# Four graph layers in one launch: where layer 1 builds the row sums for layer 2

## The chip, the cores and the metric

The kernel runs on one core of one Trainium2 chip. The metric is the device time of one launch in microseconds (us), of the slowest core, which here is the only one. Three runs of the kernel before the change took 2272.49 to 2273.15 us, with a median of 2272.7 us.

## What is computed

The input is a matrix `x` of 3327 rows of 256 numbers and an integer matrix `adj` of 3327 x 3327, of which only "greater than zero" matters. Four layers follow each other, each with a residual and a layer norm. The masked softmax over the rows of `adj` is in each of them.

```python
def _L1_gnn_ref(x, adj, W, a):
    h = x @ W
    e = (h @ a[:D, 0])[:, None] + (h @ a[D:, 0])[None, :]
    e = jnp.where(e > 0, e, 0.01 * e)
    attention = jax.nn.softmax(jnp.where(adj > 0, e, -1e12), axis=1)
    return jax.nn.elu(attention @ h)

def _L2_gnn_ref(x, adj, Wq, bq, Wk, bk, Wv, bv):
    q, k, v = x @ Wq.T + bq, x @ Wk.T + bk, x @ Wv.T + bv
    scores = q @ k.T / jnp.sqrt(d)
    attention = jax.nn.softmax(jnp.where(adj > 0, scores, -9e15), axis=-1)
    return jax.nn.elu(attention @ v)

x = _layernorm(x + _L0_gnn_ref(x, adj, Wq, Wk))       # cosine attention
x = _layernorm(x + _L1_gnn_ref(x, adj, W, a))
x = _layernorm(x + _L2_gnn_ref(x, adj, Wq, bq, Wk, bk, Wv, bv))
x = _layernorm(x + _L3_gnn_ref(x, adj, W0, W1, a1, W2, a2, W3, a3))
```

(The function bodies are shortened. Layer 0 normalizes queries and keys instead of scaling the scores. Layer 3 multiplies by `W0` and then runs three layers like layer 1, with `W1, a1` to `W3, a3`.) The change touches layer 1, the start of layer 2, and one place in layer 0.

## The kernel before

**Tiles and passes.** The rows of `x` are cut into 26 tiles of 128 rows, taken as 13 pairs. Six passes run: layers 0, 1 and 2, and the three parts 3a, 3b, 3c of layer 3. Each pass goes through seven column blocks `b`, six of four output tiles (512 columns) and a last one of two, and in each block through all 26 tiles `j`. So a step of the main loop is (layer, block, tile). In a step, ScalarE (ACT) and VectorE (DVE) make the attention weights of one tile against the block's 512 columns; TensorE (PE) multiplies them with the rows of that tile and adds the product up in five PSUM banks called `po`. In layer 1 and in 3a to 3c the weights are `re` (ACT, L786) and then `ft` or `e` (DVE, L799).

**Seven products in place of eight.** In the blocks that `strassen(L, b)` names, two tiles (a pair `p`) are multiplied by seven products of half size in place of eight (`products`, matmul at L942). Each needs four sums of the weights (`ssum`, `qsum`) and four sums of the pair's rows. The latter are the row sums of this text. `combine(key, p, v)` makes the four sums `t1` to `t4` of pair `p` for layer `key` with four VectorE operations, beside a column of ones that adds up the softmax denominator, and a DMA on SyncE's queue (SP) writes them to DRAM, `t_d[key][p]`. `fetch_tsum` (L860) loads them again for every block that uses them, into one of three buffers called `tsum`. The rows of layer 2 are the output of layer 1, so `combine("2", p)` runs inside layer 1, block by block.

**The end of a block.** When the last tile of a block has been added up, the banks are emptied: `joined` copies one of the products on ACT (`p<-po`, L968) and adds the others on DVE (`zs` L974 to L977, `p` L980 to L986). Then `finish` divides, turns the result (`planes<-p`, L1001, two copies on ACT that split the 32 bits into two planes of 16; a DMA transpose, L1004, on SP; copies of the turned planes, L1015), projects it (L1207), applies the elu (L1219), adds the residual (`y`, L1225 and L1234), and takes the layer norm. In layer 1 the normed rows come out in `o4` (L1270, on ACT) and go back into the tiles `v` of the next layer over DMAs.

**What follows it in layer 1.** In the other passes what follows is part of the block's own chain; in layer 1 it is put into a queue called `tail`, from which the main loop takes one step after each tile: `combined()`, which calls `combine("2", p)` for the two pairs of the block with a step after each and one empty step at its end; then `turn(o4, ...)`, which makes `planes<-o` on ACT (L1001), a DMA transpose on SP and, for the first four blocks, writes the turned rows to DRAM (`tr_d`, L1011), from where `turned_again` fetches them (L1029) late in layer 1 as the keys `FT` of layer 2; then `followed()`.

**Buffers.** Buffers are taken by tag, and a new user of a tag waits until an earlier one is free. Tag `x4k` has two buffers, which the `tsum` of `combine("2")` shares with the `planes` and a few others. Tag `stage` has four, `po` five banks. Tags `w_l0_wqk` and `row_1` hold the query and key weights of layer 0 and a vector of layer 1; in layer 2 two of the `ksum` tiles (pairs 1 and 2) lie there, and later weights of 3b.

**The start of layer 2.** `sum_keys(p)` (L627 to L630) makes four sums of a pair's keys, `ksum`, on DVE: some of them ahead of need, at the steps listed in `KSTEPS`, the others two steps before the pair's weights (`make`). `pair_weights` (L647 to L674) multiplies them with the sums of the queries. `masked` (L494) is the DVE operation that multiplies the finished weights of layer 2 by the mask. `weights2` (L684, L692) makes the weights of layer 2's tiles that aren't taken by pairs.

**Who sets the order.** A scheduler puts the instructions of every engine in one order, by what each depends on and by the priorities of the program; each engine then works through its own in that order and waits where an operand is missing. `tc.issue_after(i)` places what is issued in it behind instruction `i`.

## Time and profile before

The profiled execution is not one of the three runs. Its numbers beside theirs, and the stretches of the three layers concerned:

| what | value |
|---|---|
| median of three runs | 2272.7 us |
| the profiled execution | 2275.28 us |
| its span, first to last instruction | 2273.5 us |
| its mean granted TensorE clock | 0.994 |
| layer 0, 0 to 513 us: PE busy | 510.19 us |
| layer 1, 513 to 801 us: PE busy | 268.07 of 288 us |
| first 287 us of layer 2: PE busy | 285.73 us |
| `re<-u,nrh,th`, L786, ACT, all | 728 x 776 ns = 531.4 us with its smaller shapes |
| `planes<-o`, L1001, ACT | 14 x 981 ns, 19.0 us idle before them |
| `p<-po`, L968, ACT | 30 x 358 ns, 9.3 us idle before them |
| `ksum<-ft`, L627, DVE | 37 x 282 ns, 3.6 us idle before them |

How to read the views: The page gives for every engine the time in which it was busy; PEld is TensorE's loading of weights, which overlaps its matmuls. A table of stretches gives, for each stretch of time, its length and every engine's busy time with the number of instructions, then PEclk, the TensorE clock that was granted (1.00 is full speed), the busy share of the DMA engines and their rate. A line of the timeline gives start, duration, engine, source line, operation, output <- inputs, shape and number, and in brackets how long the engine stood idle before it and what ended that idle time. A line of waits gives who waited for whom, the sum, how often, and the longest. `v`, `ft`, `tsums`, `po` and so on are the program's names for tiles.

### The profile page before, as it was taken

How to read it: one execution, taken by the hardware profiler on the slowest of the kernel's cores; microseconds unless marked ns; L12 is line 12 of the kernel's file. 1: busy time of each engine (PE TensorE's matmuls, PEld its weight loads, DVE VectorE, ACT ScalarE, POOL GpSimd, SP SyncE). 2: the span in 40 equal slices, each digit the busy share in tenths (PEclk: the TensorE clock that was granted, in tenths of full speed). 3: DMA queues.
4: the chain of work that ended last, by engine and by line, in shares of the span. 5: the costliest groups of instructions: out<-in, count | busy, mean ns of one | idle time of the engine just before them, and what ended most of it. 6: DMA issues, size and time to landing. Idle time of an engine off the chain costs nothing. (4 is left out here: it accounts for less than half of the span.)

```text
span 2273.5 us, 43942 instructions
## 1 busy us (share of the span) xinstructions
PE 2225.7 (98%) x16053; PEld 2040.7 (90%) x16053; DVE 2023.7 (89%) x5495; ACT 1368.9 (60%) x2317; POOL 88.7 (4%) x256
## 2 busy tenths in 40 slices
PE   9999999999999899999999999999999999999997
PEld 7788888889999789999999999999999999899997
DVE  6789999988888778988988989999898999899997
ACT  4677777775666645445444445766565765665663
POOL 0000001000000000000000000000000000000000
PEclk9999999999999999999999999999999999999999
DMA  8655665646665622133132244656545556455542
GB/s 276 197 178 168 196 192 190 187 135 154 176 175 139 167 80 82 47 96 91 48 94 81 64 143 153 156 145 169 139 112 161 152 141 161 109 164 164 152 121 56
DMA packets 217037, 318.84 MB, mean 140 GB/s; under 512 B 95870, under 2 KB 125301, under 8 KB 212213
## 3 DMA queue, kind: packets, MB, share of 16 engines
q1 hardware_dynamic: 207908, 307.90, 46.8%
q0 software_dynamic: 8640, 7.87, 2.4%
q8 instruction: 127, 2.08, 0.4%
q14 instruction: 90, 0.73, 0.1%
q10 hardware_dynamic: 272, 0.26, 0.0%
HBM read 243.97 MB, written 40.54 MB: 125 GB/s over the span
## 5 line engine op out<-in xcount | busy, mean ns | idle before, releaser
L786 ACT ACTIVATE re<-u,nrh,th 128x512 f32<-128x512 f32 (+1 forms) x728 | 531.4, 776 | 194.5 <-DVE ft L799 160.7
L942 PE MATMUL po<-tsums,qsum 128*128 128x128 f32 (+1 forms) x3240 | 457.0, 277 | 13.3 <-ACT p L968 4.4
L799 DVE SCALAR_TENSOR_TENSOR ft<-re,rh,mask 128x512 f32<-128x512 f32 x598 | 433.5, 742 | 9.4 <-ACT re L786 7.5
L942 PEld LDWEIGHTS po<-tsums,qsum 128*128 128x128 f32 x3240 | 410.0, 194 | 15.3 <-ACT p L968 11.3
L942 PE MATMUL po<-v,ft 128*128 128x129 f32 x2392 | 365.2, 276 | 0.6 <-DVE ft L799 0.6
L942 PE MATMUL po<-tsums,ssum 128*128 128x128 f32 (+1 forms) x2142 | 326.7, 275 | 5.7 <-DMA tsums<-t_d 1.8
L942 PEld LDWEIGHTS po<-v,ft 128*128 128x128 f32 x2392 | 321.6, 192 | 5.5 <-DVE ft L799 1.0
L942 PEld LDWEIGHTS po<-tsums,ssum 128*128 128x128 f32 x2142 | 295.1, 192 | 21.5 <-issue 5.0
L942 PEld LDWEIGHTS po<-v,e 128*128 128x128 f32 x1196 | 169.3, 191 | 35.6 <-issue 23.9
L1695 PE MATMUL po<-v,e 128*128 128x257 f32 x832 | 194.2, 384 | 5.1 <-DVE zs L977 3.9
L1695 PEld LDWEIGHTS po<-v,e 128*128 128x128 f32 x832 | 157.5, 191 | 37.6 <-issue 8.9
L522 ACT ACTIVATE ex<-ps,rq 128x512 f32<-128x512 f32 (+1 forms) x183 | 118.8, 651 | 114.0 <-PE ps L509 110.9
L942 PE MATMUL po<-tsums,ft 128*128 128x128 f32 x1196 | 184.4, 276 | 0.0
L942 PE MATMUL po<-v,e 128*128 128x129 f32 x1196 | 182.3, 275 | 0.0
L509 PE MATMUL ps<-ft 128*128 128x512 f32 (+1 forms) x364 | 167.1, 564 | 0.1
L942 PE MATMUL po<-v,qsum 128*128 128x128 f32 x1080 | 165.3, 276 | 0.0
L942 PEld LDWEIGHTS po<-tsums,ft 128*128 128x128 f32 x1196 | 159.3, 193 | 0.1
L494 DVE SCALAR_TENSOR_TENSOR e<-ex,mask 128x512 f32<-128x512 f32 (+1 forms) x182 | 118.2, 650 | 41.5 <-ACT ex L674 16.5
L942 PEld LDWEIGHTS po<-v,qsum 128*128 128x128 f32 x1080 | 143.0, 193 | 0.0
L523 DVE SCALAR_TENSOR_TENSOR e<-ex,mask 128x512 f32<-128x512 f32 (+1 forms) x183 | 116.1, 642 | 27.8 <-ACT ex L522 27.4
L465 DVE CUSTOM_DVE_ANT_0 acc<-acc,stage 128x1024 uint16<-128x1024 uint16 (+1 forms) x168 | 108.4, 645 | 10.9 <-DMA stage<-in_adj_a 9.0
L647 PE MATMUL ps<-gsums,ksum 128*128 128x256 f32 x408 | 112.4, 382 | 1.0 <-ACT ex L658 0.7
(332 smaller groups left out, 3752.7 us busy)
## 6 DMA issues: line engine op xcount, KB each, us to landing
tsums<-t_d SPq DMA_DIRECT2D x217, 256.5 KB
mask<-mask_d SPq DMA_DIRECT2D x30, 1664.0 KB
stage<-in_adj_a SPq DMA_DIRECT2D x78, 512.0 KB
tsums<-t3a_d SPq DMA_DIRECT2D x77, 256.5 KB
tsums<-t3b_d SPq DMA_DIRECT2D x77, 256.5 KB
tsums<-t3c_d SPq DMA_DIRECT2D x77, 256.5 KB
mask_d<-mask SPq DMA_DIRECT2D x6, 1664.0 KB
xsum<-v POOLq DMA_DIRECT2D x60, 128.0 KB, 4.3
```

The costliest lines, as they stand in the source:

```text
L465: nc.vector.tensor_tensor(acc, acc, st[:, h * wd : (h + 1) * wd], ALU.add)
L494: nc.vector.scalar_tensor_tensor(e[:, :wd], t_[:, :wd], 0.0, mask(b, j), ALU.add, ALU.mult)
L509: nc.tensor.matmul(ps[:, :wd], FT[j // 4][:, 0, (j % 4) * P : (j % 4 + 1) * P], FT[b][:, 1, :wd], start=True, stop=True,)
L522: nc.scalar.activation(t_[:, c], ps[:, c], AF.Exp, scale=rq[:, j : j + 1])
L523: nc.vector.scalar_tensor_tensor(e[:, c], t_[:, c], 0.0, mask(b, j)[:, c], ALU.add, ALU.mult)
L647: nc.tensor.matmul(out, l, r, start=first, stop=True, skip_group_check=True)
L786: a_ = nc.scalar.activation(t_[:, :wd], self.u[b][:, :wd], AF.Relu, bias=self.nrh[:, j : j + 1], scale=self.th[:, j : j + 1],)
L799: v_ = nc.vector.scalar_tensor_tensor(e[:, :wd], t_[:, :wd], self.rh[:, j : j + 1], mask(b, j), ALU.add, ALU.mult,)
L942: nc.tensor.matmul(o, x, y, start=(p == 0 and g not in banks[:i]), stop=(p == NT // 2 - 1 and g not in banks[i + 1 :]),)
L1695: nc.tensor.matmul(pos[k], e[:, k * P : (k + 1) * P], V[L.i % 2][i], start=(i == 0), stop=(i == NT - 1),)
```

## The change

It has three parts.

1. The row sums of layer 2, except those of the last pair (which stay on chip), take their buffers from the tags `w_l0_wqk` and `row_1` in turn, and not from `x4k`. The order inside is now `t2, t3, t4, t1`, ones, so that the column of ones comes last, for all layers. The buffer holds only the four sums, and the DMA writes only these; the ones of the twelve pairs are written into `t_d["2"]` once, by twelve DMAs of 128 x 1 numbers that are issued in block 3 of layer 0. The memset of the ones on DVE is left out; the last pair's goes to GpSimd (POOL).
2. The empty step at the end of `combined()` is left out, so that `turn(o4)` begins a step sooner.
3. The key sums of layer 2's block 0, both those of `KSTEPS` and those made two steps ahead, are placed behind the last mask multiplication (`masked`) that was issued before them.

```diff
@@ -488,10 +488,12 @@
         nc.vector.tensor_scalar(am[:, :n], am[:, :n], 0.0, 0.5, ALU.is_gt, ALU.mult)
         anyadj[b] = am
 
+    last_masked = [None]
+
     def masked(b, j, t_):
         wd = bw(b)
         e = work.tile([P, CH], F32, tag="e", name="e", bufs=9)
-        nc.vector.scalar_tensor_tensor(
+        last_masked[0] = nc.vector.scalar_tensor_tensor(
             e[:, :wd], t_[:, :wd], 0.0, mask(b, j), ALU.add, ALU.mult
         )
         return e
@@ -833,25 +835,28 @@
 
         b1, b2 = v[2 * p], v[2 * p + 1]
         b11, b12, b21, b22 = b1[:, H:D], b1[:, :H], b2[:, H:D], b2[:, :H]
-        if (key, p) in kept or key in ("0", "1"):
+        if key == "2" and (key, p) not in kept:
+            t = wts.tile([P, 4 * H], F32, tag=("w_l0_wqk", "row_1")[p % 2], name="tsum")
+        elif (key, p) in kept or key in ("0", "1"):
             t = work.tile([P, 4 * H + 1], F32, tag="tsum", name="tsums", bufs=3)
         else:
             t = work.tile([P, 4 * H + 1], F32, tag="x4k", name="tsum", bufs=2)
         if (key, p) in kept:
             tsums[kept[key, p], p] = t
-        t1, t2, t3, t4 = (t[:, c : c + H] for c in (0, H + 1, 2 * H + 1, 3 * H + 1))
+        t2, t3, t4, t1 = (t[:, c : c + H] for c in range(0, 4 * H, H))
         if e is None:
-            (nc.vector if key == "2" else nc.gpsimd).memset(t[:, H : H + 1], 1.0)
+            if key != "2" or (key, p) in kept:
+                nc.gpsimd.memset(t[:, 4 * H :], 1.0)
             nc.vector.tensor_tensor(t1, b12, b11, ALU.subtract)
             nc.vector.tensor_tensor(t3, b22, b12, ALU.subtract)
         else:
-            one = t[:, H : H + 1]
+            one = t[:, 4 * H :]
             nc.vector.tensor_scalar(one, e[:, :1], 0.0, None, ALU.is_ge)
             nc.vector.scalar_tensor_tensor(t1, b12, one, b11, ALU.mult, ALU.subtract)
             nc.vector.scalar_tensor_tensor(t3, b22, one, b12, ALU.mult, ALU.subtract)
         nc.vector.tensor_tensor(t2, b22, t1, ALU.subtract)
         nc.vector.tensor_tensor(t4, t2, b21, ALU.subtract)
-        nc.sync.dma_start(t_d[key][p], t)
+        nc.sync.dma_start(t_d[key][p][:, : t.shape[1]], t)
 
     fetched = [None]
 
@@ -920,10 +925,10 @@
             1: b1[:, H:],
             2: b2[:, H:],
             3: b2[:, :H],
-            4: t[:, 3 * H + 1 :],
-            5: t[:, : H + 1],
-            6: t[:, H + 1 : 2 * H + 1],
-            7: t[:, 2 * H + 1 : 3 * H + 1],
+            4: t[:, 2 * H : 3 * H],
+            5: t[:, 3 * H :],
+            6: t[:, :H],
+            7: t[:, H : 2 * H],
         }
 
         for k, i in (
@@ -1309,7 +1314,6 @@
                 for k in range(0, n, 2):
                     combine("2", (ts_[0] + k) // 2, {t: o4[:, i, :] for i, t in enumerate(ts_)})
                     yield
-                yield
 
             if L.key == "1":
                 if b < NB - 1:
@@ -1502,7 +1506,8 @@
         if j % 2 == 0 and s + 2 < len(steps):
             ln, bn, jn = steps[s + 2]
             if by_pairs(ln, bn, jn // 2) and jn // 2 not in ksum:
-                now[bn, jn // 2] = sum_keys(jn // 2)
+                with tc.issue_after(last_masked[0].ins) if bn == 0 else ExitStack():
+                    now[bn, jn // 2] = sum_keys(jn // 2)
         done = inner.popleft() if j % 2 and inner else None
         if done:
             next(done)
@@ -1736,6 +1741,8 @@
         begin = 14
         if L.is_gat and b < NB - 1:
             begin = 2 if last and b == NB - 2 else 10
+        if L.key == "0" and b == 3 and j < NT // 2 - 1:
+            nc.sync.dma_start(t_d["2"][j][:, 4 * H :], ones[:, :1])
         if L.key == "0" and b == NB - 1 and j % 6 == 0 and 0 < j < 24:
             combine("1", j // 6 - 1, V[1])
         if L.key == "1" and j % 4 == 1 and j < (24, 12, 0, 0, 0, 0, 0)[b]:
@@ -1749,7 +1756,8 @@
                         again.remove(g)
         if L.key == "2" and b * NT + j in KSTEPS:
             p = KSTEPS[b * NT + j]
-            ksum[p] = sum_keys(p)
+            with tc.issue_after(last_masked[0].ins):
+                ksum[p] = sum_keys(p)
         if L.key == "2" and (b, j) == (0, 3):
             sum_queries(0)
         if j == (25 if L.key == "1" else 22) and not end:
```

## The prediction, made before the changed kernel was run

> **What bounds the kernel now.** I read the page first, then the table of stretches, then TensorE's waits, then the timeline around the longest of them, and last the groups by line.

> ```profile
> PE 2225.7 (98%) x16053; PEld 2040.7 (90%) x16053; DVE 2023.7 (89%) x5495; ACT 1368.9 (60%) x2317; POOL 88.7 (4%) x256
> ```

> TensorE (PE) is busy for 98% of the span, so only work taken from it, a gap in it, or a slow clock can change the time. No matmul is added or removed. The gaps are 47.8 us in all, so I looked for those the change can touch: layer 1, from about 513 to 790 us.

> ```profile
> core 0: us, PE busy (x) PEld busy (x) DVE busy (x) ACT busy (x) POOL busy (x), PEclk, DMA share, GB/s
> 563.34:613.78 50.44, 47.10 (x388) 46.36 (x389) 43.21 (x107) 31.40 (x46) 3.13 (x4) 0.97 0.65 175
> 613.78:663.34 49.56, 46.68 (x384) 45.92 (x385) 43.40 (x106) 31.79 (x46) 2.57 (x3) 0.97 0.66 170
> 663.34:710.51 47.17, 44.34 (x380) 43.76 (x381) 43.17 (x106) 31.49 (x46) 4.29 (x5) 1.00 0.65 164
> 710.51:760.90 50.39, 46.51 (x375) 45.46 (x375) 39.65 (x102) 28.92 (x45) 2.58 (x3) 0.97 0.67 169
> 760.90:801.18 40.28, 36.71 (x134) 26.21 (x135) 31.20 (x119) 28.23 (x45) 2.58 (x3) 0.96 0.53 144
> ...
> 1501.15:1545.36 44.21, 44.21 (x384) 43.77 (x383) 42.18 (x97) 29.22 (x46) 3.64 (x6) 1.00 0.61 164
> ...
> 1797.09:1842.70 45.61, 45.60 (x393) 44.98 (x393) 43.02 (x99) 29.77 (x47) 3.63 (x6) 1.00 0.63 153
> ```

> The first four rows are full column blocks of layer 1, cut where TensorE restarts after a block change. The last two are blocks of layers 3a and 3b with the same products. Layer 3a needs 44.21 us; layer 1 needs 47 to 50.

> ```profile
> PE po L942 <- ACT p L968: 4.4, 2, 2.8
> PE po L1695 <- DVE zs L977: 3.9, 1, 3.9
> PE po L942 <- DVE p L980: 3.4, 1, 3.4
> PE po L942 <- DVE zs L977: 2.8, 1, 2.8
> PE po L942 <- DMA tsums<-t_d: 1.8, 2, 1.3
> ```

> These are TensorE's waits from 540 to 765 us. Four rows, 14.5 us, wait for the same thing: a bank of the finished block (`po`) that ScalarE (ACT) must copy (L968) and VectorE (DVE) must add to before the next block may write it. The timeline shows why that copy is late:

> ```profile
> 559.07 0.83 PE L942 MATMUL po<-v,ft 128*128 128x129 f32 x6
> ...
> 560.40 1.99 ACT L1001 COPY planes<-o 128x1024 uint16<-128x1024 uint16 x2 [4.20 <-DMA t_d<-tsum]
> ...
> 562.29 0.36 ACT L968 COPY p<-po 128x256 f32<-128x256 f32 x1
> ...
> 563.34 1.76 PE L942 MATMUL po<-tsums,qsum 128*128 128x128 f32 x8 [3.43 <-DVE p L980]
> ```

> The next fence is the same place of a block change in layer 3a, and the one after it a stretch of one microsecond after the change near 611 us, with the columns of the table above.

> ```profile
> 1504.99 0.37 ACT L968 COPY p<-po 128x256 f32<-128x256 f32 x1 [0.59 <-PE po L942]
> ...
> 1507.24 0.83 PE L942 MATMUL po<-v,ft 128*128 128x129 f32 x6
> ```

> ```profile
> 616.00:617.00 1.00, 1.00 (x6) 1.00 (x6) 1.00 (x3) 0.80 (x2) 0.00 (x0) 0.50 1.07 186
> ```

> ACT stands in order. `planes<-o` waits 4.20 us because its slot (tag `x4k`, two buffers) is still being read by the DMA that writes `tsum` to DRAM. The L968 copy stands behind it. In layer 3a no such copy is in front: L968 runs 2.25 us before the next block's first matmul, and TensorE has no gap. The same picture repeats near 610, 661, 708 and 757 us, with TensorE gaps of 2.83, 1.56, 2.83 and 3.88 us. The row at 616 shows a second cost: after the gaps at 560, 610, 708 and 757 the granted clock is 0.50 for 3 to 4 us, some 1.5 to 1.9 us lost each; after the 1.56 us gap it stays 1.00.

> **The change, part by part.**

> *Places of their own for layer 2's row sums.* `planes<-o` loses its DMA wait (19.0 us of ACT idle time in the group's row, six times). In the built order it also stands two to five `re` activations earlier, ahead of L968. ACT has room: before 560 us it sat idle for 2.18 us ahead of the last two `re`. So L968 should start when its bank is complete, as in layer 3a. First block change: minus 3.43. The four periods sum to 197.56 us. What an unblocked one takes is bounded by 44.21 (3a) and 45.61 (3b, which holds a transfer wait). Layer 1 has its own measure: the third row started without a slow clock, and 47.17 less its final gap of 2.83 is 44.34. The first two rows, less gap, tsums wait (0.51, 1.31) and 1.75 of clock, give 45.35 and 44.94. I take 44.9: 197.56 - 179.6 = 18.0 us gained, bounds 15.1 (all at 45.61) and 20.7 (all at 44.21). VectorE fits: 43.4 us of work per block, as in layer 3a, so it nearly becomes the bound.

> *The last block of layer 1* (760.90 to 801.18). It is only two tiles wide, so TensorE has little to do while the finished block runs L968, `planes<-p`, transpose, `pT`, projection: L968 at 759.81 to the first projection at 774.35 is 14.5 us, and VectorE and ACT pace it. L968 cannot start before five more `re` of 0.6 us, about 2 us after the last full block's end (754.4) instead of 5.4, so up to 2.7 us of the 3.88 gap may stay. But one `elu_e` now stands one 1.3 us copy earlier on ACT, and VectorE no longer holds key sums in this stretch (one stood 2.88 us waiting for a copy of `ft`, with the others about 5 us of work). The gain is between 0 and 6.5 us (TensorE's own work here is 33.8 us); I take 3.0, nearer the lower end because the chain, not TensorE, paces it.

> A gap left at that change has a price in clock: the 2.83 us gaps were each followed by 3 us at 0.50, so I count 1.6 us for a gap of 2.7, inside the 3.0. [...]

> *Planes a step sooner.* One empty step is gone per block. It issues two ACT copies (0.99 us each) and one DMA transpose on SP sooner; that transpose now stands before the next fetches of `tsums`, one or two places earlier in SP's order. SP's transposes take 1.24, 2.08 and 5.27 us (least, median, most). The fetch behind it went out at 556.89 for a pair needed 3.1 us after the block change, 563.0: a lead of 6.1 us against a landing of about 2.7 (fetch at 604.0, TensorE released at 606.7). At 2.08 us it is hidden, at 5.27 it costs 2 us. I take 0; the 44.9 leaves 0.5 for it.

> *Key sums behind the weights.* About 32 VectorE additions (0.28 us, 0.2 apart) move from 770-794 into layer 2's first block. From 800 to 840 VectorE was busy 30.5 of 40 us, partly idle because ACT waited on planes (3.45 and 1.94 us idle). It stays under 40, so 0, bounds -1 to +2. TensorE's wait of 0.78 us for L692 at 814 us, also behind planes, should go: 0.3 net.

> *Memsets.* Twelve of 0.06 us leave VectorE and one moves to POOL (0.1 us, 4% busy): 0.

> *Ones in DRAM.* Twelve DMAs of 128 x 4 bytes on SP. The built order puts them among layer 0's adjacency loads near 60 to 75 us, and one load falls behind two stores of row sums, about 4 us. TensorE shows 60.00 of 60 us busy there although VectorE waited 3.6 us for such loads: covered. I take 0; the bounds are 0 and 12 x 4.3 us (the `xsum` DMA's landing time, the only one shown) = 51.6, if they ran one by one and nothing covered them.
> [...]

> Sum: 3.4 + 18.0 + 3.0 + 0.3 = 24.7 us. The profiled execution took 2275.3 us (span 2273.5), 2.6 above the median of 2272.7; taken from the median: **2248 us**.

> **Rivals.**

> *Fetches late behind the moved transposes.* For: SP is in order, and at the first and fourth block change three fetches stand behind the transpose. Against: median 2.08 us. At 2 us on each of five changes the gain is 14.7: 2258.

> *The last block gives time back.* For: its chain is longer than TensorE's work. If the 3.0 is nothing and 2.7 us of gap with 1.6 of clock come on top of today's waits, the gain is 17.4: 2255.

> *Slower: the twelve DMAs starve layer 0.* At the full 51.6 us, less some 19 us that the four buffers of loads cover (a load each 4.7 us), 32.6 reach TensorE: 2272.7 - 24.7 + 32.6 = 2281. It decides only from 24.7 us past the cover. Against: nothing suggests that these run one by one; the loads on the same queue overlap.

> *It doesn't do what it says:* `planes` waits for another user of its slot, and L968 stays late: 2272. Against: the slot's earlier users finish 10 us or more before.

> **How the numbers follow.** Forecast 0.66, late fetches 0.14, last block 0.12, slower 0.04, no effect 0.04. The forecast's own range: gains of 18 (15.1 + 3.4, nothing else) to 30 (20.7 + 3.4 + 6.5, less 1), 2242 to 2255. Reaching to the first rival and some of it beyond: 2242 to 2261. About 0.2% (4.5 us) is what a measurement can tell from no change; the cases give 0.92 faster, 0.04 same, 0.04 slower.

> **What would show it.** Right: `planes<-o` with no wait for `t_d<-tsum`; L968 before the block's last matmul; layer 1 periods of 44 to 46 us; granted clock 1.00 through them; first layer 2 products about 24 us earlier. Wrong: TensorE waiting on `tsums<-t_d` for over 1.5 us at the changes, a gap over 2 us before the projection in the last block, or gaps before 120 us.

## The result, and the profile after

| | before | after |
|---|---|---|
| median | 2270.5 us (12 runs, 2266.5 to 2275.9) | 2264.6 us (12 runs, 2260.3 to 2269.6) |
| profiled execution | 2275.3 us | 2264.4 us |
| ratio after / before | | 0.9973, 95% interval 0.9961 to 0.9984 |

The change makes the kernel 3.6 to 8.9 us faster. The forecast was 24.7 us, a time of 2248.0 us in a range of 2242 to 2261.

What the change was to remove is gone. The row of the planes' group, all layers, before (L1001) and after (L1006), gives busy time, mean ns of one, and the idle time before them:

```profile
L1001 ACT COPY planes<-o 128x1024 uint16<-128x1024 uint16 (+1 forms) x14 | 13.2, 981 | 19.0 <-DMA t_d<-tsum 19.0
```

```profile
L1006 ACT COPY planes<-o 128x1024 uint16<-128x1024 uint16 (+1 forms) x14 | 13.1, 976 | 0.0
```

TensorE's waits from 540 to 765 us in the profile after (who waited for whom, us in total, times, longest):

```profile
PE po L947 <- DMA tsums<-t_d: 10.5, 8, 2.3
PE pproj L1212 <- DVE pT L1020: 2.0, 1, 2.0
```

`planes<-o` waits for nothing (19.0 us before), and no wait for a bank of the finished block is left (14.5 us before). In their place TensorE waits eight times, 10.5 us, for row sums fetched from DRAM, for which it waited 1.8 us before. The new kernel's lines are five further down after the changed functions: L942 is L947, L968 is L973, L1015 is L1020, L1288 is L1293. Blocks are counted from 0, as in the program, and a place is written block.pair. Block 0 of layer 1 isn't taken by pairs and runs before the 513 us from which the tables count layer 1; blocks 1 to 5 are taken by pairs, and block 6 is the narrow last one. The "first block change" is the one from block 1 to block 2.

Both programs issue the same 16053 matmul records, in nearly the same order, so the same record can be compared in both. The table of stretches below is cut at such records: the first two rows are before, from TensorE's start in block 2 to a matmul early in layer 1's last block (the one that waited 3.88 us before the change, so that this gap lies in the first row), and from there well into layer 2 (pair weights running); the other two are the same work after.

```profile
563.34:760.90 197.56, 184.63 (x1527) 181.50 (x1527) 169.44 (x418) 123.59 (x183) 12.58 (x15) 0.97 0.66 170
760.90:838.15 77.25, 72.90 (x358) 56.78 (x359) 59.20 (x205) 45.39 (x79) 2.58 (x3) 0.98 0.41 110
```

```profile
560.42:752.81 192.39, 181.85 (x1528) 178.50 (x1527) 170.52 (x414) 122.31 (x185) 13.75 (x16) 0.99 0.69 177
752.81:827.86 75.05, 72.21 (x359) 56.89 (x358) 53.38 (x173) 44.69 (x78) 1.72 (x2) 0.98 0.40 110
```

| step of the sum | forecast | measured in the two profiles |
|---|---|---|
| up to layer 1 (twelve DMAs of ones) | 0 | -0.7 |
| first block change | 3.4 | 3.6 |
| four block periods | 18.0 | 197.56 - 192.39 = 5.2 |
| last block, and L692 in layer 2 | 3.3 | 77.25 - 75.05 = 2.2 |
| the rest of the kernel | 0 | 0.3 |
| sum | 24.7 | 10.6 |

The step that failed is the periods. Why a fetch is late shows in the timeline of SP and ACT after, near 650 us, with TensorE's wait behind it:

```profile
646.20 2.06 ACT L1275 ACTIVATE o<-y,nm,rstd 128x256 f32<-128x256 f32 x4
646.81 2.03 SPq L1293 DMA_DIRECT2D v<-o  x2
...
648.95 0.53 SPq L865 DMA_DIRECT2D tsums<-t_d  x1
...
652.27 0.98 PE L947 MATMUL po<-tsums,ssum 128*128 128x128 f32 x3 [2.28 <-DMA tsums<-t_d]
```

The fetch of pair 3.12 needs a buffer, which TensorE freed at 642.6 us (the last matmul of pair 3.9 on `tsums`). It goes out at 649.5. Between the two, SP stands at the stores of the normed rows `v<-o`, which wait for ACT's `o` (L1275). TensorE uses a pair up in 3.1 us, and with three buffers a fetch that leaves at once is out 6.9 us before TensorE wants it (pairs 3.10 and 3.11). This one was out 0.5 us before TensorE wanted it (649.99), and TensorE started 2.8 us after the issue. In the profile before, the stores stand at the same place in SP's order. After the change TensorE wants pair 3.12 6.6 us sooner (656.63 before), but ACT begins `o` only 4.8 us sooner (650.98), and the fetch is out only 3.9 us sooner.

A second kind of lateness, near the first block change, first before and then after:

```profile
556.89 0.43 SPq L860 DMA_DIRECT2D tsums<-t_d  x1
562.41 2.01 SPq L1004 DMA_TRANSPOSE turned<-planes  x1
```

```profile
554.07 1.04 ACT L1006 COPY planes<-o 128x1024 uint16<-128x1024 uint16 x1
...
556.84 4.19 SPq L1009 DMA_TRANSPOSE turned<-planes  x1
...
561.12 1.93 SPq L865 DMA_DIRECT2D tsums<-t_d  x3
```

```profile
565.26 0.94 PE L947 MATMUL po<-tsums,qsum 128*128 128x128 f32 x6 [1.55 <-DMA tsums<-t_d]
```

The transpose of `planes<-o` now goes out at the block change, 4.19 us long, ahead of three fetches; before, the first of these (pair 2.1) was ahead of it. The transposes of `planes<-o` at the five block changes hold SP for 1.79 to 2.67 us in the profile before and for 3.75 to 5.11 us in the one after; why they take longer isn't shown.

A third kind stands near 740 us, where the mask of a block (1664 KB) goes out right ahead of a fetch:

```profile
736.67 0.32 SPq L425 DMA_DIRECT2D mask<-mask_d  x1
737.10 0.37 SPq L865 DMA_DIRECT2D tsums<-t_d  x1
```

That fetch (pair 5.11) was out 5.65 us before TensorE wanted it, and TensorE still waited 1.85 us: it started 7.5 us after the issue, against 2.8 to 4.1 us for the other seven. Before, this mask went out after the block's last fetch. By place, the eight waits are 4.7 us behind stores (0.91, 0.51, 2.28, 0.99), 4.0 behind transposes (1.55, 0.40, 2.06), and 1.85 behind the mask.

### The profile page after: what moved, and what is told of

Same layout as the page of the kernel before. It is cut to its first block, busy times and chain, and to the rows that moved or that the text cites. A ratio compares the mean times of both kernels' runs of the same rounds, so it can differ in the third digit from the quotient of the medians.

```text
span 2262.6 us, 43919 instructions
## 1 busy us (share of the span) xinstructions
PE 2221.0 (98%) x16053; PEld 2035.4 (90%) x16053; DVE 2022.4 (89%) x5482; ACT 1368.2 (60%) x2317; POOL 87.9 (4%) x257
## 3 DMA queue, kind: packets, MB, share of 16 engines
q8 instruction: 127, 2.08, 0.4%
## 5 line engine op out<-in xcount | busy, mean ns | idle before, releaser
L788 ACT ACTIVATE re<-u,nrh,th 128x512 f32<-128x512 f32 (+1 forms) x728 | 531.0, 776 | 191.8 <-DVE ft L801 156.0
L947 PE MATMUL po<-tsums,qsum 128*128 128x128 f32 (+1 forms) x3240 | 451.9, 275 | 9.8 <-DMA tsums<-t_d 7.4
L801 DVE SCALAR_TENSOR_TENSOR ft<-re,rh,mask 128x512 f32<-128x512 f32 x598 | 433.3, 742 | 14.7 <-ACT re L788 13.0
L947 PEld LDWEIGHTS po<-tsums,qsum 128*128 128x128 f32 x3240 | 405.5, 192 | 12.2 <-DMA tsums<-t_d 6.0
L947 PE MATMUL po<-v,ft 128*128 128x129 f32 x2392 | 365.3, 275 | 0.7 <-DVE ft L801 0.6
L947 PE MATMUL po<-tsums,ssum 128*128 128x128 f32 (+1 forms) x2142 | 328.4, 276 | 8.5 <-DMA tsums<-t_d 3.2
L947 PEld LDWEIGHTS po<-v,ft 128*128 128x128 f32 x2392 | 321.4, 192 | 5.8 <-DVE ft L801 1.0
L947 PEld LDWEIGHTS po<-tsums,ssum 128*128 128x128 f32 x2142 | 296.4, 192 | 24.6 <-issue 5.0
L947 PEld LDWEIGHTS po<-v,e 128*128 128x128 f32 x1196 | 169.3, 191 | 35.6 <-issue 23.7
L947 PE MATMUL po<-tsums,ft 128*128 128x128 f32 x1196 | 183.0, 275 | 0.0
L947 PE MATMUL po<-v,e 128*128 128x129 f32 x1196 | 182.3, 275 | 0.0
L947 PE MATMUL po<-v,qsum 128*128 128x128 f32 x1080 | 164.9, 275 | 0.0
L947 PEld LDWEIGHTS po<-tsums,ft 128*128 128x128 f32 x1196 | 158.0, 192 | 0.2
L947 PEld LDWEIGHTS po<-v,qsum 128*128 128x128 f32 x1080 | 142.3, 192 | 0.0
L465 DVE CUSTOM_DVE_ANT_0 acc<-acc,stage 128x1024 uint16<-128x1024 uint16 (+1 forms) x168 | 108.5, 646 | 12.6 <-DMA stage<-in_adj_a 10.6
```

The source lines that it names most:

```text
L465: nc.vector.tensor_tensor(acc, acc, st[:, h * wd : (h + 1) * wd], ALU.add)
L788: a_ = nc.scalar.activation(t_[:, :wd], self.u[b][:, :wd], AF.Relu, bias=self.nrh[:, j : j + 1], scale=self.th[:, j : j + 1],)
L801: v_ = nc.vector.scalar_tensor_tensor(e[:, :wd], t_[:, :wd], self.rh[:, j : j + 1], mask(b, j), ALU.add, ALU.mult,)
L947: nc.tensor.matmul(o, x, y, start=(p == 0 and g not in banks[:i]), stop=(p == NT // 2 - 1 and g not in banks[i + 1 :]),)
```

## The experiments

Two theories were set against each other. Theory A: SP works through its queue in order, and the fetches are late because they stand behind stores that wait for ACT and behind transposes. Theory B: layer 1 now runs faster, the same bytes crowd the DMA engines, and every landing is later. Eleven runs were made, on different chips; ratios are to the kernel before on the same chip.

**The parts of the change.** `old_step` puts the empty step back:

```diff
                     combine("2", (ts_[0] + k) // 2, {t: o4[:, i, :] for i, t in enumerate(ts_)})
                     yield
+                yield
```

> The changed kernel with the empty step at the end of combined() put back, so that planes and their transpose come a step later again; own places and queued key sums stay. Theory A (SyncE's queue is in order, and fetches of row sums stand behind the moved transposes and behind stores that wait for ScalarE): the waits of 1.55, 0.40 and 2.06 us at pairs 1, 2 and 1 of blocks 2, 3 and 5 (4.0 us) go, the others (some 6.5 us) stay; 2 to 5 us faster than the changed kernel if the copy L968 is not late again. Theory B (layer 1 now runs faster, so the same bytes crowd the DMA engines and every landing is later): TensorE's waits for tsums stay at 9 to 11 us wherever the transposes stand; within 1 us of the changed kernel.

Ratio 0.9956 (0.9940 to 0.9972), which overlaps the change's own. The waits at pairs 2.1 and 3.2 fell to 0.87 and 0, but the one at 5.1 stayed (2.01), and the sum was 8.7 us. In the trace, SP issues the same DMAs in the same order as in the changed kernel in layer 1, and TensorE and ACT the same work; of DVE's operations two neighbours change places. So it isn't the step that moves the transposes ahead of the fetches. The prediction of theory A for this run (these waits go) failed, since the edit doesn't touch what A names.

`no_keys` takes part 3 out:

```diff
-                with tc.issue_after(last_masked[0].ins) if bn == 0 else ExitStack():
-                    now[bn, jn // 2] = sum_keys(jn // 2)
+                now[bn, jn // 2] = sum_keys(jn // 2)
...
-            with tc.issue_after(last_masked[0].ins):
-                ksum[p] = sum_keys(p)
+            ksum[p] = sum_keys(p)
```

> The changed kernel with layer 2's key sums where they were (not queued behind the masked weights). Both theories: layer 1 up to its last block as in the changed kernel (waits for tsums 9 to 11 us). If the queueing is worth the 2.2 us that the last block gained, 785 to 830 us is that much longer, with VectorE's key sums and a wait for gq or y again; if it is worth nothing, within 1 us of the changed kernel.

Ratio 0.9971 (0.9957 to 0.9984); tsums waits 8.9 us. With the key sums back in their old place, TensorE still has no wait at `pgq`, layer 2's first product (2.3 us before the change), and the work of the last block's row in the table takes 74.5 us (75.05 in the changed kernel). So the wait hung on the late end of the block ahead of it (0.6 us of it are left in `places_only`).

`places_only` is part 1 alone, with both edits above:

> Part 1 of the change alone: own places for the row sums and ones in DRAM, with the old step and the old key sums. Theory A: waits for tsums of 5 to 7 us, no wait of planes for t_d<-tsum; as fast as the changed kernel or up to 3 us faster. Theory B: waits for tsums of 9 to 11 us; as the changed kernel, or up to 2 us slower for the key sums.

Ratio 0.9976 (0.9960 to 0.9992). It has the whole effect of the change, within the intervals: planes wait for nothing, and SP's order in layer 1 is again that of the changed kernel. The view gives 9.4 us of waits for `tsums` up to 765 us, and 2.8 us at pairs 3.0 and 5.0 that it puts down to DVE; but these two waits, which hang on a fetch too, end within 0.03 us of the fetch's last landing (607.49 and 700.65), so that the waits for row sums are some 12 us and none for a bank is shown. Theory A's 5 to 7 us, which expected the old order with the old step, were missed. So the new places alone bring the gain, and they alone move the transposes.

`sooner_only` and `keys_only` are parts 2 and 3 on the kernel before.

> The kernel before with part 2 of the change alone: the empty step of combined() left out. If the step sooner moves planes and transposes (as the forecast had it): planes still wait for t_d<-tsum, L968 stays late, and fetches may be later; 0 to 3 us slower. Rival: the scheduler's order hardly hangs on that step; same time as the kernel before within 1.5 us, with the same gaps at the block changes.

Ratio 1.0016 (1.0006 to 1.0026): 1 to 6 us slower, though SP's order in layer 1 is that of before and the same banks are waited for. Its profile has five steps of 3.41 us at half clock in layer 1, where those of the kernel before have four; the fifth accounts for 1.7 us in that profile. Together with the lower ratio of `old_step` this suggests that part 2 costs time; how isn't shown.

> The kernel before with part 3 alone: layer 2's first key sums behind the masked weights. If it is worth the 2 us that the last block of layer 1 gained in the changed kernel: TensorE's wait of 1.9 to 2.3 us at gq goes, 1 to 2 us faster than the kernel before. Rival: that wait hangs on the late end of the block before; same time within 1 us.

Ratio 1.0000 (0.9989 to 1.0011), with a wait of 1.7 us at `pgq` as before.

**How typical the profiles were.** `before_again` and `after_again` are the two kernels themselves, on one chip.

> The kernel before, profiled once more, to see how typical its first profile was (2275.3 us; the median is some 5 us lower). If the forecast's base was typical: again about 12.5 us of waits for the banks of the finished block and four stretches of slow clock in layer 1. If not: the same five waits for the banks, but 2 to 5 us less in all.

2270.4 us. The same places wait for the same banks. Over the same matmuls, from some 487 to 838 us in the first profile, TensorE's gaps of over 0.2 us are 17.2 us in sum against 20.6 there; the slow clock took as long (13.7 us in layer 1). The four periods took 195.97 us, not 197.56. So the first profile was not quite typical.

> The changed kernel on the same chip as the others of this call. Theory A: waits for tsums at the same pairs as before (2.1, 2.12, 3.12, 5.0, 5.1, 5.11, counted block.pair), 8 to 12 us, since SyncE's order is fixed in the program. Theory B: about as much in all, but at other pairs. 5 to 7 us faster than the kernel before.

2260.5 us (four runs, 2260.1 to 2261.1) against 2268.6 for the kernel before: 8.1 us faster, ratio 0.9962 (0.9947 to 0.9977). The waits came at pairs 2.1, 2.12, 3.0, 3.2, 3.12, 5.0, 5.1 and 5.11, the same eight as in the first profile, 10.5 us again. (The view lists 9.0 us in seven waits, and puts the 1.5 us at pair 5.0 down to DVE; the fetch's last landing, at 700.23, is 0.02 us before the end of that wait.) The four periods took 190.84 us, 5.1 less than in `before_again`, as the first two profiles have it (5.2). A fixed order would give the same pairs each time. That alone doesn't rule out theory B, as the same bytes move at the same places; the next run does.

**SP's order or the DMA engines.** `stores_pool` issues the same stores from another engine:

```diff
-                    nc.sync.dma_start(nxt[t][:, :D], dsts[k])
+                    nc.gpsimd.dma_start(nxt[t][:, :D], dsts[k])
```

> The changed kernel with the stores of layer 1's normed rows (v<-o) issued by GpSimd in place of SyncE. Theory A: the waits of 0.91, 0.51, 2.28 and 0.99 us behind these stores (4.7 us, and the slow clock after the 2.28, 1.7 us) go, those behind the transposes (4.0) stay; 4 to 6 us faster than the changed kernel. Theory B: the same bytes move, waits for tsums stay at 9 to 11 us; no change, or slower by GpSimd's issues of 0.9 us each.

Ratio 0.9942 (0.9924 to 0.9960), 2255.6 us against 2267.4. Its timeline near 642 us, and TensorE's waits from 540 to 765 us:

```profile
641.88 0.32 SPq L865 DMA_DIRECT2D tsums<-t_d  x1
641.91 2.06 ACT L1275 ACTIVATE o<-y,nm,rstd 128x256 f32<-128x256 f32 x4
642.80 2.18 POOL L1293 DMA_DIRECT2D v<-o  x4 [22.62 <-ACT o L1275]
```

```profile
PE pproj L1212 <- DVE pT L1020: 2.7, 1, 2.7
PE po L947 <- DMA tsums<-t_d: 2.5, 3, 1.6
PE po L947 <- ACT p L973: 1.5, 1, 1.5
```

The same bytes move, POOL waits for `o` in SP's place, and the fetch goes out while `o` is still being made. Of 10.5 us of waits 2.5 are left, and the four periods take 184.82 us, not 192.39. Those behind transposes went too, which A had not expected: the transpose ahead of pair 2.1 no longer stands behind the stores and goes out at 554.19, not 556.84, so that the fetch behind it was issued 3.7 us after its buffer came free, and 5.7 in the changed kernel. Theory B, that every landing is late, falls. Its idea holds for the three waits that are left: at pairs 2.12, 5.11 and 5.12 the fetch was issued in time, 6.1 to 8.8 us before TensorE wanted it, and a mask had gone out just ahead.

`mask_late` places the loads of the masks behind the last fetch issued:

```diff
-            masks[nb] = fetch_mask(nb)
+            with tc.issue_after(fetched[0].ins) if L.key == "1" else ExitStack():
+                masks[nb] = fetch_mask(nb)
```

> The changed kernel with layer 1's loads of the next block's mask (1.6 MB) placed behind the fetch of row sums that was issued last before them, so that none goes out right ahead of pair 5.11. Theory A and the mask as a third cause: the wait of 1.85 us at pair 5.11 goes, whose fetch was issued in time and landed after 7.5 us; the others stay; 1 to 2 us faster than the changed kernel, or less if the weights then wait for the mask. If the mask has nothing to do with it: the wait at 5.11 stays.

Ratio 0.9952 (0.9937 to 0.9967); 2259.1 us (2255.0 to 2259.8) against 2260.5 for the changed kernel on that chip (2260.1 to 2261.1): 1.4 us, from four runs each. The wait at 5.11 is gone, as expected, with its fetch now out ahead of the mask. But the others did not stay: those at 2.12, 3.2, 3.12 and 5.1 are gone, those at 3.0 and 5.0 grew to 3.06 and 1.95, one came at 4.0, and two came for weights (2.0 us). In the profiles the four periods are 4.0 us shorter than in `after_again` and the last block 3.3 us longer. That the sum comes out in the expected 1 to 2 us is luck, since the edit changes SP's order at more places than pair 5.11.

`all_moved` is `stores_pool` and `mask_late` together, and the stores of layer 2's row sums issued by POOL too:

```diff
-        nc.sync.dma_start(t_d[key][p][:, : t.shape[1]], t)
+        (nc.gpsimd if key == "2" else nc.sync).dma_start(t_d[key][p][:, : t.shape[1]], t)
```

> The changed kernel with the stores of layer 1's normed rows and of layer 2's row sums issued by GpSimd, and with the mask loads placed as in mask_late. Theory A: waits for tsums under 1.5 us in all of layer 1, no slow clock before the last block; 12 to 16 us faster than the kernel before, 1 to 3 us more than with the stores of the rows alone. Theory B: waits for tsums of 9 to 11 us.

2253.8 us (2252.7 to 2257.0) against 2268.6 for the kernel before and 2260.5 for the changed one on the same chip; ratio to before 0.9934 (0.9918 to 0.9951). It beats both kernels. Its four periods take 184.58 us, with 3.8 us of waits in them; without these it is 180.8, close to the forecast's 179.6. Its waits from 540 to 765 us:

```profile
PE po L947 <- ACT p L973: 2.2, 2, 1.3
PE pproj L1212 <- DVE pT L1020: 1.5, 1, 1.5
PE po L947 <- DMA tsums<-t_d: 1.3, 1, 1.3
PE po L947 <- DVE p L987: 0.5, 3, 0.2
```

`turn_late` also puts the transposes of `planes<-o` behind the fetch issued last:

```diff
+        with tc.issue_after(fetched[0].ins) if late else ExitStack():
-        nc.sync.dma_start_transpose(
+            nc.sync.dma_start_transpose(
...
+                        late=b < NB - 2,
```

> all_moved with the transposes of planes<-o in blocks 0 to 4 placed behind the fetch of row sums issued last before them. Theory A: the wait of 1.3 us at pair 2.1, whose fetch stands behind such a transpose, goes; 1 to 2 us faster than all_moved, 14 to 17 us faster than the kernel before. Rival: the waits left over are for the banks of the finished block (L968 behind re on ScalarE), so the 1.3 us only moves; within 1 us of all_moved.

Ratio 0.9939 (0.9924 to 0.9954), as `all_moved` on another chip; 12.6 us faster than the kernel before, not 14 to 17. No wait for `tsums` is left from 540 to 765 us; the waits for the banks rose from 2.2 to 3.1 us, and TensorE waited 1.3 us for a weight `ft`. The waits speak for the rival: once the fetches are in time, the copy of the finished bank, behind `re` on ACT, ends last again. The times can't tell 1 to 2 us from none, as the interval is some 7 us wide. A fourth buffer for the fetches was not tried, so how far it alone would have gone is open.

## Why the prediction was wrong

**What bounds layer 1, and the first block change.** Right. `planes<-o` waited for its slot and held L968 back; with a slot of its own it doesn't, and L968 starts at 557.50, 2.9 us before TensorE turns to the next block's row sums (560.42) without a gap. 3.6 us, forecast 3.4 (3.0 between the second profiles).

**The step that failed** is in the working of "planes a step sooner": the late fetches of row sums were given "I take 0; the 44.9 leaves 0.5 for it", and the two waits of 0.51 and 1.31 us for `tsums` were taken out of the first two periods before they were averaged to 44.9. What the forecast removed did go: 12.9 us of gaps and 5.1 of slow clock lie in the four periods before, and its 4 x 44.9 = 179.6 leaves them out. But 10.5 us of waits for fetches and 1.7 of slow clock after the longest of them came instead. Together that is 191.8, against 192.39 measured. So the term that was put at 0 measured 12.2 us.

The forecast had looked at one fetch, that of pair 2.1. When it is needed was right (563.0; 563.71 in the profile after, which is 0.7 later from layer 0 on), and so was the new order. The size was not: it took the median of all the kernel's transposes, 2.08 us, and the one ahead of this fetch took 4.19. The fetch was out 1.6 us before it was needed, not 6.1, landed after 3.2, and cost 1.55 us; the forecast's own "at 5.27 it costs 2 us" was nearer. The fetches behind stores that wait for `o` (4.7 us, and the slow clock) and behind the mask (1.85) it put at nothing without a reason. Two of them showed in the profile before, as the waits of 0.51 and 1.31 at pairs 2.12 and 3.12. They should have been kept and made larger: without the gaps TensorE comes sooner, and `o` comes sooner by less, as the numbers at pair 3.12 show. `stores_pool` shows SP's order to be the cause of 8.0 of the 10.5 us. Why the transposes take twice as long after the change stays open.

**The rival "fetches late behind the moved transposes"** had the right resource and a part of the places: transposes account for 4.0 of the 10.5 us, and the stores `v<-o` for 4.7, which no rival named. That its price of 10 us is close to the 10.5 is luck. That the step moves the transposes, as the prediction had it, was wrong (`old_step`, `places_only`).

**The base.** The forecast took gaps from one execution of 2275.3 us and subtracted them from the median. The second profile of the kernel before, at 2270.4, is 4.9 us faster, 1.6 of it in the same four periods. The first profiles of the two kernels stand 10.6 us apart at the last matmul; the medians 6.0, and 8.1 on the chip of the second ones. Of the 18.7 us between the forecast gain and that of the medians, 12.8 are the periods, 1.1 the last block, and 4.6 this difference between profiles and medians.

**The last block** gained 2.2, forecast 3.0 and 0.3. The gap at its start (3.88, counted with the periods) went in whole, where the forecast had left up to 2.7 us of it: the copy L968 (now L973) ran at 747.95, before the block's last products and not about 2 us behind them. In its place a wait of 1.97 us for `pT` came at the projection, with a slow clock after it. That this is about the 2.7 and 1.6 that the forecast left for the gap is luck. The key sums had no part in this (`no_keys`, `keys_only`).

**The twelve DMAs of ones** cost nothing that can be seen: against the first profile of before, the thousandth matmul comes between 1.0 us later and 1.2 us sooner in the nine profiles with them, and 0.2 to 0.7 us sooner in the three without them.

## What to carry to other kernels

The gaps that were removed here brought the busiest engine forward, and not by as much what the queue that feeds it waits for: at pair 3.12, TensorE by 6.6 us and ACT's `o` by 4.8. For each transfer that is needed behind it, work out when it goes out in the new order, with the lengths of what stands just ahead of it at that place and not a median over the whole kernel, and keep a small wait that shows already.
Keep stores that wait for an engine out of the queue that feeds the busiest engine. Moved to POOL's queue here (POOL is busy for 4% of the span), they took 8.0 us of waits away (`stores_pool`); with the stores of the row sums moved and the masks put later too, the gain was 6.7 us on top of the change's 8.1 on the same chip.
SP's order changed with the buffers and not with the step that was to change it, so the order should be read for each edit alone.

## What the hardware showed

In the first profiles of the two kernels the slow clock goes by a fixed grid and not by the length of a gap alone. In the profile after, two stretches have half clock before the program's end, and these rows (the table of stretches) show one of them and a place after a gap of 2.06 us that has none:

```profile
652.20:655.20 3.00, 2.92 (x14) 2.96 (x15) 0.35 (x1) 1.14 (x3) 0.00 (x0) 0.50 1.05 265
707.70:710.70 3.00, 3.00 (x27) 3.00 (x28) 3.00 (x6) 3.00 (x5) 0.50 (x1) 1.00 0.89 284
```

Stores on SP that waited for ACT held up the fetches behind them: the fetch of pair 3.12 went out 6.9 us after its buffer came free (642.6 to 649.5 in the profile after), and `stores_pool`, where the stores wait elsewhere, has 8.0 us less of waits.
